# The mask term of 32 attention sets, added by two engines in place of one

## The chip, the cores and the metric

The kernel runs on one core of one Trainium2 chip. A core has five instruction queues that matter here: TensorE (PE, its weight loads are shown as PEld), VectorE (DVE), ScalarE (ACT), GpSimd (POOL) and SyncE (SP), which issues the DMAs. Each engine works through its queue in order; semaphores hold an instruction until what it needs is there. The metric is the device time of one execution in microseconds (us), as the median of several runs.

## The reference

Four cross-attention blocks follow each other on an array of 32 sequences, 64 rows each, 256 features. Blocks 0 to 2 are an 8-head attention without a mask, a 16-head attention with a boolean mask, and a latent attention with an integer mask and an MLP (those two masks come in through PE). Block 3 is a decoder layer: masked self-attention, masked cross-attention, and an MLP, all with 16 heads of 16 features. Only its two attentions use the mask in this form:

```python
def attention(q, k, v, mask):
    scores = jnp.einsum('bhqd,bhkd->bhqk', q, k) / jnp.sqrt(jnp.float32(HD))
    scores = scores * mask - 10000.0 * (1.0 - mask)
    probs = jax.nn.softmax(scores, axis=-1)
    return jnp.einsum('bhqk,bhkd->bhqd', probs, v)
```

The self-attention takes one mask of 64 x 64 for all sequences, the cross-attention one mask of 64 x 64 for each sequence. Everything is float32.

## The kernel before

Block 0 is written out by hand and runs until about 458 us. The three attentions after it and block 3's second one are cut into 80 *sets*: a set is two sequences (128 rows, on the partitions) with all 16 heads, or half the heads where the keys are twice as many. Sets 0 to 47 are of kind `k`, sets 48 to 63 of kind `s` (block 3's self-attention) and sets 64 to 79 of kind `x` (its cross-attention). Sets `s` and `x` are the masked ones, 32 in all.

`attend(n)` (line 1388) emits the work of set n. For a masked set this is: PE computes the scores into four PSUM banks (`a_scores`, tile `s`, of which there is one); DVE multiplies them by the mask on the way to SBUF (tile `E`, 128 x 1024, three of them), and POOL adds the second term, (mask - 1) x 10000, in place (`a_mask`, line 1026); DVE takes the largest of each row and head (`a_max`, tile `mx`); it is subtracted by DVE or POOL in turn (`a_sub`); ACT takes the exponential; DVE sums and inverts (`a_sum`, tile `sm`); PE turns the result, multiplies it with the values, and DVE scales the product (`a_fin`, tile `rb`), with ACT and POOL splitting it into a high and a low part (`xTho`, `xTlo`). The mask and its term are 64 columns wide and are read again for each of the 16 heads: `m3` and `c3` (tiles `m`, `c`) for kind `s`, computed once; `mk` and `ck` for kind `x`, loaded and computed for each set.

Between the sets, steps with due times prepare the keys, values and queries of later sets, the norms, the output projections, the MLP, and the weights (`norm_steps`, `mlp_steps`, `load_unit`). Some of them use DVE and POOL as well: `x<-pj,x` (adding a projection to the rows), `x<-x,row` (adding a bias row, POOL), `xTl`, `xTla`, `xTlh`, `xTln` (the low parts of transposed rows; DVE or POOL), `rstd` and `nmr` (norms, POOL), `w` and `wraw` (weights).

From set 0 on, the order of all instructions is computed when the kernel is built. Class `Plan` collects every operation, joins PE's neighbouring ones on one bank to *atoms*, and makes one atom of each operation of the other engines (`link`, line 254). `order` (line 289) then places the atoms one by one on the engine that can start first; where several could start, the smallest `urgent` goes first: the due time of the atom, plus a random number up to 0.5, less 3 for a DVE or ACT atom that reads PSUM. The random numbers are drawn one for each atom in the order of emission, from a fixed seed. The costs come from `cost` (line 194); of two lines that matter here the first is DVE's with both inputs in SBUF and the second is POOL's (w is the width in columns):

```python
return 0.3 + w * (1.05e-3 if o.method in ("tensor_copy", "tensor_scalar") else 1.3e-3), 0.05, None
...
return 0.1 + w * (2.45e-3 if three and not self.repeats(ins[1]) else 1.95e-3), 0.05, None
```

The operations are issued from one place (`write`, line 123), so in the profile almost all of them have line L125; L156 is the same for block 0. They are told apart by their tiles, written out<-in,in.

Of the kernel before, what the change touches and what calls it, by code (L numbers as in the profile page):

```python
# [15 lines left out]
ALU = mybir.AluOpType  # L16
# [3 lines left out]
P = 128  # L20
# [388 lines left out]
def mk_kernel(ctx: ExitStack, tc: tile.TileContext, a: dict, out: bass.AP):  # L409
    nc = tc.nc  # L410
    plan = Plan(dict(V=nc.vector, A=nc.scalar, G=nc.gpsimd, T=nc.tensor, S=nc.sync))
    V, A, G, T, SY = [plan.engine(k) for k in "VAGTS"]
# [613 lines left out]
    def a_mask(u):  # L1026
        if u["kind"] == "x":
            G.tensor_scalar(u["ck"], u["mk"], -1.0, 10000.0, ALU.add, ALU.mult)
        else:
            u["mk"], u["ck"] = m3, c3  # L1030
        spread = lambda t: t.unsqueeze(1).unsqueeze(1).broadcast_to([P, 4, 4, 64])
        V.tensor_tensor(u["ev"], u["src"], spread(u["mk"]), ALU.mult)
        G.tensor_tensor(u["ev"], u["ev"], spread(u["ck"]), ALU.add)
        u["src"] = u["ev"]

    def a_max(u):
# [351 lines left out]
    def attend(n):  # L1388

        for x in steps:  # L1390
            if x["due"] <= n:
                run(x)
        plan.due = n + 0.5
        for gen in loads.get(n, ()):
            next(gen)
        u = sets[n]
        for nme in (f"q{u['l']}{u['g']}", f"v{u['l']}{u['g']}" + ("1" if u["two"] else "")):
            run(by_name[nme])
        plan.due = n
        a_mask_load(u)  # L1400
        a_scores(u)
        if u["kind"] != "k":
            a_mask(u)
        a_max(u)
        a_sub(u)
        a_exp(u)
        a_sum(u)
        a_scale(u)
        a_rows(u)
        a_turn(u, 0)  # L1410
        a_turn(u, 1)
        a_values(u)
        a_fin(u)
# [261 lines left out]
```

## Time and profile before

| | |
|---|---|
| median of three runs | 1131.25 us (1130.16 to 1131.29) |
| the profiled execution | 1132.07 us |
| its span, first to last instruction | 1130.3 us |
| mean granted TensorE clock | 0.987 |
| busy: PE / PEld | 1067.8 (94%) / 872.2 us (77%) |
| busy: DVE / ACT / POOL | 894.9 (79%) / 906.3 (80%) / 761.8 us (67%) |
| POOL `E<-E,c` and `E<-E,ck`, 128 x 1024 | 16 and 16, median 2.38 and 2.39 us |
| DVE `E<-s,m` and `E<-s,mk`, 128 x 1024 | 16 and 16, median 1.22 and 1.21 us |

Busy time is the time in which an engine executes; it says nothing of the order. A group of the profile is all instructions with the same engine, operation, tiles and shape. "Idle before" is the time in which the engine stood still just before an instruction, with the engine that ended the wait. The chain of waits starts at the last instruction and goes back, at each step to what released it, so that it tells which engine set the time in each part of the span.

### The profile page before, as it was taken

Reading aid. Unit: us, or ns where it says so; the run is one execution under the profiler, and the core shown is the slowest. Engines: PE = TensorE matmul, PEld = TensorE weight load, DVE = VectorE, ACT = ScalarE, POOL = GpSimd, SP = SyncE. Lnnn points to the kernel's source line nnn. Section 1 sums busy time; section 2 is a strip of 40 time slices with the busy share of each in tenths; the row PEclk is TensorE's granted clock in tenths of the full one; section 3 lists DMA queues with packets and bytes.
Section 4 is the critical chain, followed back from the end, with each engine's and each line's share of the span. In section 5 each row is a group of like instructions: output and inputs, shape, how many; then the busy total and the mean of one; then the engine's idle time right before and its main releaser. Section 6 shows DMA issues by size and latency. Waiting matters only on the chain.

```text
span 1130.3 us, 35569 instructions
## 1 busy us (share of the span) xinstructions
PE 1067.8 (94%) x14396; PEld 872.2 (77%) x14396; DVE 894.9 (79%) x1575; ACT 906.3 (80%) x2326; POOL 761.8 (67%) x829
## 2 busy tenths in 40 slices
PE   6999999999999999899999999999999988889998
PEld 4666666666666666788898989998988877779998
DVE  4889989897888777688888878777878878777842
ACT  2888888887888789577778889889898777888974
POOL 3788888886778667635546634477866989996520
PEclk9999999999999999899999999999999989989999
DMA  3001211111110100311211100000000111110000
GB/s 96 21 25 36 61 35 49 35 34 44 34 34 25 34 16 2 93 37 58 68 47 47 34 26 26 21 29 22 21 20 21 49 51 51 43 34 21 11 20 29
DMA packets 41300, 41.21 MB, mean 36 GB/s; under 512 B 7059, under 2 KB 37796, under 8 KB 41136
## 3 DMA queue, kind: packets, MB, share of 16 engines
q1 hardware_dynamic: 40816, 38.54, 10.9%
q8 instruction: 114, 1.87, 0.7%
q10 hardware_dynamic: 320, 0.40, 0.1%
q14 instruction: 50, 0.41, 0.1%
HBM read 26.30 MB, written 2.10 MB: 25 GB/s over the span
## 4 chain that ended last, share of the span: by engine, by line
PE 59%; DVE 15%; ACT 10%; POOL 10%; issue 4%; DMA 0%; SPq 0%; DVEq 0%; POOLq 0%; ACTq 0%
PE pj L125 39%; PE pt L156 6%; ACT E L156 5%; PE av L156 5%; PE sc L156 4%; PE s L125 4%; DVE mx L156 3%; POOL E L125 3%; DVE E L125 2%; DVE PT L156 2%; ACT PT L156 2%; DVE sB L156 2%; POOL E L156 2%; DVE mx L125 2%; PE pt L125 1%
## 5 line engine op out<-in xcount | busy, mean ns | idle before, releaser
L156 POOL TENSOR_TENSOR E<-E,rs 128x512 f32<-128x512 f32 x256 | 263.5, 1040 | 84.0 <-DVE rs L156 64.5
L156 ACT ACTIVATE E<-sc,mx 128x256 f32<-128x256 f32 x512 | 238.4, 481 | 23.2 <-DVE rs L156 21.9
L156 DVE TENSOR_REDUCE mx<-sc 128x4 f32<-128x1024 f32 x128 | 155.8, 1217 | 2.8 <-PE sc L156 1.4
L156 PE MATMUL sc<-cd,T 64*128 64x256 f32 x1024 | 144.0, 400 | 10.5 <-ACT E L156 10.0
L125 POOL TENSOR_TENSOR E<-E,sm 128x512 f32<-128x512 f32 x96 | 101.1, 1078 | 68.9 <-DVE sm L125 56.1
L156 PE MATMUL av<-PT,us 128*64 128x256 f32 x1024 | 125.0, 385 | 0.0
L156 PEld LDWEIGHTS pt<-ident,E 64*128 64x128 f32 x2048 | 83.6, 139 | 43.6 <-POOL E L156 15.8
L156 PEld LDWEIGHTS av<-PT,us 128*64 128x64 f32 x1024 | 68.3, 136 | 54.7 <-issue 20.4
L156 PEld LDWEIGHTS sc<-cd,T 64*128 64x128 f32 x1024 | 89.6, 189 | 25.8 <-ACT E L156 17.8
L125 DVE TENSOR_REDUCE sm<-E 128x16 f32<-128x1024 f32 (+1 forms) x80 | 96.0, 1200 | 15.3 <-ACT E L125 15.3
L156 ACT ACTIVATION_READ_ACCUMULATOR E<-sc,mx 128x1 f32 x512 | 108.0, 211 | 0.0
L156 PE MATMUL pt<-ident,E 64*128 64x64 f32 x2048 | 98.2, 228 | 6.1 <-ACT PT L156 2.2
L125 ACT COPY PTe<-pj 128x512 f32<-128x512 f32 x160 | 88.0, 590 | 19.2 <-PE pj L125 17.1
L125 PE MATMUL pj<-ident,E 128*128 128x128 f32 x640 | 90.8, 281 | 8.0 <-DVE rb L125 2.5
L156 ACT COPY PT<-pt 128x512 f32<-128x512 f32 x128 | 75.6, 591 | 24.3 <-PE pt L156 22.8
L125 PE MATMUL pj<-w,xThh 128*128 128x256 f32 x512 | 93.4, 287 | 0.1
L125 PE MATMUL pj<-xThn,w 128*128 128x256 f32 x512 | 92.2, 285 | 0.7 <-DVE rb L125 0.4
L156 DVE COPY PT<-pt 128x512 f32<-128x512 f32 x128 | 86.0, 672 | 5.2 <-PE pt L156 5.1
L125 ACT ACTIVATE E<-E 128x1024 f32<-128x1024 f32 x80 | 84.9, 1062 | 5.8 <-DVE E L125 4.6
L125 PEld LDWEIGHTS pj<-ident,E 128*128 128x128 f32 x640 | 71.6, 143 | 16.7 <-issue 3.6
L125 DVE TENSOR_TENSOR xTlh<-u,xThh 128x512 fp32r<-128x512 f32 x64 | 54.8, 861 | 29.9 <-ACT xThh L125 29.5
L156 DVE RECIPROCAL rs<-sm 128x2 f32<-128x2 f32 x256 | 40.1, 156 | 46.5 <-ACT E L156 43.7
(223 smaller groups left out, 2798.3 us busy)
## 6 DMA issues: line engine op xcount, KB each, us to landing
kb<-kfm SPq DMA_DIRECT2D x44, 128.0 KB
xd<-in_x SPq DMA_DIRECT2D x32, 128.0 KB
cd<-in_ctx SPq DMA_DIRECT2D x32, 128.0 KB
boot<-in_ctxT SPq DMA_DIRECT2D x16, 256.0 KB
kb<-kfm SPq DMA_DIRECT2D x64, 64.0 KB
xt<-in_x SPq DMA_DIRECT2D x16, 128.0 KB
boot<-in_ctx SPq DMA_DIRECT2D x8, 256.0 KB
out<-x SPq DMA_DIRECT2D x8, 256.0 KB
```

The lines of the kernel that those rows point to most:

```text
L125: getattr(self.engines[o.key], o.method)(*[real(x) for x in o.p], **{k: real(x) for k, x in o.k.items()})
L156: return f(*p, **k)
```

## The change

The second term of the mask is added in two instructions in place of one. The tile `E` is seen as 4 groups x 4 heads x 64 keys, so its 1024 columns are divided by the first of these: the first three quarters, 768 columns, are added by POOL (`G`), and the last quarter, 256 columns, by DVE (`V`). DVE's instruction is emitted first. The multiplication before it and all else stay; the operation count grows by one DVE operation for each of the 32 masked sets.

```diff
-        spread = lambda t: t.unsqueeze(1).unsqueeze(1).broadcast_to([P, 4, 4, 64])
+        spread = lambda t, n=4: t.unsqueeze(1).unsqueeze(1).broadcast_to([P, n, 4, 64])
         V.tensor_tensor(u["ev"], u["src"], spread(u["mk"]), ALU.mult)
-        G.tensor_tensor(u["ev"], u["ev"], spread(u["ck"]), ALU.add)
+        V.tensor_tensor(u["ev"][:, 3:4], u["ev"][:, 3:4], spread(u["ck"], 1), ALU.add)
+        G.tensor_tensor(u["ev"][:, 0:3], u["ev"][:, 0:3], spread(u["ck"], 3), ALU.add)
         u["src"] = u["ev"]
```

## The prediction

> **What bounds the kernel now.** I read four views in this order: the page's busy shares, the busy times by stretch, the chain of work that ended last, and the groups and the timeline of the instructions that the change touches.
>
> The masked sets are the last 32 of the 80 sets that the planner orders, and their multiplications (DVE, `E<-s,m` and `E<-s,mk`) start between 785 and 1056 us. So I cut the end of the span into stretches, with one stretch of layer 0 to compare with. The columns are the stretch, its length, and busy us of PE, PEld, DVE, ACT and POOL.
>
> ```profile
> 60.00:250.00 190.00, 182.87 (x2003) 122.16 (x2003) 171.75 (x367) 160.85 (x558) 160.87 (x185) 1.00 0.14 41
> ...
> 785.00:880.00 95.00, 91.44 (x1387) 83.99 (x1370) 77.35 (x102) 84.16 (x169) 69.08 (x62) 1.00 0.05 19
> 880.00:990.00 110.00, 96.42 (x1376) 85.03 (x1374) 87.80 (x148) 86.68 (x185) 104.30 (x103) 0.93 0.16 50
> 990.00:1062.00 72.00, 68.42 (x915) 63.44 (x916) 58.19 (x72) 61.19 (x113) 54.70 (x49) 0.96 0.07 22
> ```
>
> The reader is to see three different limits. I call the last three rows A, B and C. In A, PE is busy 96% and is the limit; DVE is at 81%, POOL at 73%. In B, PE falls to 88% (13.6 us idle) and POOL is at 95%: B is bound by POOL. In C, PE is back at 95%. PE's idle time is 3.6 + 13.6 + 3.6 = 20.8 us: that is all that the change could ever win, since it takes nothing from PE. After 1062 us no masked set is left, and PE runs almost alone to the end.
>
> The chain of waits says the same of B. It runs mostly over POOL from 878.78 to 933.75 (with two turns over DVE and PE) and from 948.12 to 990.77 us; this is a piece of it (start, us, what):
>
> ```profile
> 961.50 2.40 POOL E L125
> 963.90 1.67 POOL xTlo L125
> 965.96 0.71 POOL rstdm L125
> 966.95 0.71 POOL rstda L125
> 967.74 0.50 POOL nmrm L125 x2
> 968.25 1.86 POOL E L125
> 970.20 0.25 POOL ck L125
> 970.52 2.38 POOL E L125
> 972.90 1.24 POOL x L125
> ```
>
> The 2.40 and the 2.38 are the additions that the change divides. Nine such additions of about 2.3 to 2.4 us, and one with 0.8 us of it, lie on these two runs of the chain.
>
> **The change part by part.** It edits one line, so every masked set (16 `s`, 16 `x`) is touched once: one POOL instruction becomes shorter, one DVE instruction is new, and the reduction `mx<-E` waits for both. No DMA, no tile and no PE work changes.
>
> *POOL, shorter.* Three rows of two-input POOL operations have three widths: `xTlo<-rb,xTho` 256 columns, median 0.74 us; `x<-x,row` 512 columns, 1.29 us; the addition itself, 1024 columns, 2.38 us (`c`) and 2.39 us (`ck`). They lie on a line of 2.15 ns a column, so 768 columns take 1.84 us. **Saved: 0.55 us a set**, 17.6 us for 32.
>
> *DVE, new.* The trace has no addition of 256 columns with both inputs in SBUF. `rb<-pj,rb` has this width with one input in PSUM: 0.41 us. DVE's two-SBUF-input `E<-E,mx` of 1024 columns takes 1.16 us when nothing is in its way, `xTlh` of 512 takes 0.68; that line also goes through 0.41. So 0.41 us undisturbed. But the same rows show that it will seldom be undisturbed:
>
> ```profile
> L125 DVE TENSOR_TENSOR E<-E,mx 128x1024 f32<-128x1024 f32 x16 | 30.2, 1890 | 0.3
> ```
>
> That is the group (16 instructions, 30.2 us busy, mean 1890 ns); and from the timeline (start, us, engine, operation):
>
> ```profile
> 808.48 3.45 DVE L125 TENSOR_TENSOR E<-E,mx 128x1024 f32<-128x1024 f32 x1
> ...
> 808.43 2.41 POOL L125 TENSOR_TENSOR E<-E,c 128x1024 f32<-128x1024 f32 x1
> ...
> 863.15 2.08 DVE L125 TENSOR_TENSOR E<-E,mx 128x1024 f32<-128x1024 f32 x1
> ...
> 864.11 1.73 POOL L125 TENSOR_TENSOR xTlo<-rb,xTho 128x256 fp32r<-128x256 f32 x1
> ```
>
> At 808.48 DVE starts a subtraction just after POOL's addition, and takes 3.45 us: the 2.36 us that POOL still ran, and then 1.09, its own undisturbed time. At 863.15 it waits 1.0 us for a POOL addition to end, runs 1.08, and now POOL's next instruction, started at 864.11, takes 1.73 in place of 0.74: it waited in turn. So where these two engines meet, a DVE operation with two SBUF inputs and a POOL operation run one after the other, and the later one stands at the head of its queue. The 16 `E<-E,mx` have a mean of 1.89 us, 0.73 us above the undisturbed one. That mean wait depends on POOL's instruction and not on DVE's width, so I give it to the new addition too: 0.41 + 0.73 = **1.14 us of DVE a set**. Ends: 0.41 when it runs first (it follows the multiplication on the same engine, while POOL's addition began 0.08 us after the multiplication's end in the sets where POOL was free); 0.41 + 1.84 = 2.25 when it always stands behind its own set's POOL addition. 1.14 is nearest to a measured row of the same operation kind.
>
> *POOL, waiting in return.* Each DVE addition holds POOL up to 0.41 us if POOL has something to run. In B it nearly always has (95%): 0.55 - 0.41 leaves 0.14 us a set. In A and C POOL has slack, and neither the gain nor the wait reaches the end.
>
> *A rule.* The Trainium skill, "GPSIMD Engine Reference", section Engine selection, puts elementwise work on VectorE because GpSimd is about twice as slow with two inputs; by that alone the sum would be the relief of the first rival below. The same page, section Key points, says that the two share SBUF interfaces and contend when a VectorE instruction has two SBUF inputs; it gives no price, this trace does (3.45 us against 1.16).
>
> *The new wait.* `mx<-E` now waits for two engines. Behind it in DVE's queue stand drains of PSUM (`rb`, `x<-pj,x`, `xTla`) for which ACT and then PE wait. In A and C the multiplication is followed on DVE by 3 to 12 other instructions before `mx<-E`, so DVE, not the addition's end, sets the time of most reductions there. A shorter addition wins nothing there.
>
> *The order.* The instruction order is computed: `cost` would now charge POOL 1.98 in place of 2.61 us and DVE 0.63 us more for the set (its formula gives 0.63 where I expect 1.14), and `order` draws one random tie-breaker for each atom, so every atom emitted after the first new one draws another number. Before 785 us the order stays almost as it is. The 346 us after it are re-dealt; I can't price that from the trace except by PE's idle time there, and I use it as width, some 3 us either way.
>
> *Sum by stretch.* A, 11 sets: DVE goes from 77.35 to 77.35 + 12.5 = 89.9 of 95 us, 95%. Two bounds: layer 0's stretch above has DVE at 90% beside PE at 96%, so nothing lost; B has an engine at 95% beside 12.3% of PE idle against A's 3.7%, so 8.2 us lost. I take a quarter of it, **+2.0**, because only 5 points of DVE separate A from the stretch that loses nothing. C, 7 sets: DVE 58.19 + 8.0 = 66.2 of 72, 92%; bounds 0 and (12.3 - 5.0)% of 72 = 5.3 us; a quarter, **+1.3**. B, 14 sets: POOL 14 x 0.14 = **-2.0** (ends: -7.7 without any wait, 0 with it and nothing saved on the chain). DVE gains 16.0 and stands at 103.8 of 110, 94%, as full as POOL is now. In its middle it is worse:
>
> ```profile
> 920.00:960.00 40.00, 33.82 (x562) 29.51 (x546) 33.97 (x55) 32.37 (x70) 38.96 (x36) 0.96 0.16 51
> ```
>
> Five multiplications start in these 40 us: DVE's 33.97 becomes 39.7 of 40. DVE has 6.0 us idle there, much of it waiting for others, and it works in order; I take 2.5 us of that as kept, **+2.5** (ends 0 and 6.0). Sum: 2.0 + 1.3 - 2.0 + 2.5 = **+3.8 us**. The profiled execution took 1132.07 (span 1130.3 and 1.77 around it), so 1135.9; it lay 0.8 above the median of the runs, 1131.25, so the forecast is **1135** for the median. About 0.2%, 2.3 us, is what a measurement of this kernel can tell from no change.
>
> **The rivals.**
> *POOL's relief decides.* For it: B's chain is POOL, and the additions on it are its longest pieces; if the DVE additions run first, in gaps, the chain loses 10 x 0.55 = 5.5 us (7.7 if all 14 count), and PE has 13.6 us idle there to give back. Against it: DVE meets POOL at work in B. 1131.25 - 5.5 = **1126**, 1122 to 1129. Chance 0.32.
> *No change.* PE in A and C hides everything, B's relief and DVE's load cancel: **1131**, 1129 to 1133.5. Chance 0.16.
> *DVE is stopped by its own set's addition.* Both halves become ready at the same moment. If POOL mostly starts first, a DVE addition takes 2.25 us, 72 us for 32, where DVE has 277 - 223.3 = 53.7 us idle from 785 to 1062. From about 1.7 us each (54 / 32) DVE alone is the bound of all three stretches: at 2.25 it is 18 us over, at 2.0 some 10. **1141** to 1149. Chance 0.12.
> *It doesn't do what it says.* POOL's time might not fall with the width; the three widths on one line speak against it. It is inside "no change".
>
> **How the numbers follow.** Forecast (slower, DVE's waits): 0.40, its own range 1133.5 to 1140. Faster is the first rival, 0.32. Within 0.2%: 0.16. Slower: 0.40 + 0.12 = 0.52. The range goes from 1123 (the first rival with most of its relief) to 1143 (the stopped DVE at its lower end), which leaves out about 0.15.
>
> **What would show it.** POOL's `E<-E,c` and `E<-E,ck` of 768 columns: 1.84 us when undisturbed, up to 2.25 behind DVE. The new DVE addition: a mean near 1.14, a smallest near 0.41. DVE in A near 90 us, POOL in B near 101. In the chain from 880 to 990, DVE where POOL stood. I am wrong if the new addition's mean is near 0.5 (then the first rival) or near 2 (then the last), or if PE's idle time in A and C doesn't grow although DVE does.

## The result and the profile after

The changed kernel takes 1138.78 us in the median of six runs (1136.13 to 1139.57), the kernel before 1131.51 in six runs beside them: a ratio of 1.0062, 95% interval 1.0051 to 1.0073. It is 7 us slower; the forecast was 4 us slower. The profiled execution took 1138.98 us with a span of 1137.3.

The stretches of the prediction, for the changed kernel (length, then busy us of PE, PEld, DVE, ACT, POOL, then the granted clock):

```profile
785.00:880.00 95.00, 89.64 (x1323) 81.32 (x1324) 85.20 (x117) 82.36 (x165) 64.25 (x65) 1.00 0.05 19
880.00:990.00 110.00, 97.16 (x1474) 85.38 (x1472) 99.34 (x147) 86.74 (x184) 101.74 (x100) 0.95 0.17 52
990.00:1062.00 72.00, 67.26 (x920) 60.98 (x912) 60.23 (x87) 59.65 (x116) 47.47 (x51) 1.00 0.06 18
1062.00:1138.00 76.00, 68.53 (x632) 66.74 (x620) 31.06 (x52) 45.18 (x88) 13.69 (x20) 0.94 0.06 22
```

DVE has 7.9, 11.5 and 2.0 us more than before in A, B and C, and POOL 4.8, 2.6 and 7.2 us less. PE idles 5.4, 12.8 and 4.7 us where it idled 3.6, 13.6 and 3.6. The stretches have fixed times and not the same work: what is not done in one comes in the next. In the last row, after the masked sets, PE is busy for 68.5 us and idle for 6.8 of the 75.3 us to the end of the span; before, it was busy for 64.5 and idle for 3.9 of 68.3:

```profile
1062.00:1131.00 69.00, 64.45 (x625) 63.31 (x623) 28.91 (x50) 42.39 (x87) 13.43 (x20) 0.98 0.07 24
```

The halves of the addition (smallest, median and largest time in ns of 16 each):

```profile
L125 POOL TENSOR_TENSOR E<-E,c x16: 1815/1853/2104, 787.7 to 917.7; 128x768 f32<-128x768 f32 x16
L125 DVE TENSOR_TENSOR E<-E,c x16: 384/443/1515, 788.4 to 907.1; 128x256 f32<-128x256 f32 x16
...
L125 DVE TENSOR_TENSOR E<-E,ck x16: 361/417/1873, 924.0 to 1065.7; 128x256 f32<-128x256 f32 x16
L125 POOL TENSOR_TENSOR E<-E,ck x16: 1810/1834/2206, 928.3 to 1059.1; 128x768 f32<-128x768 f32 x16
```

POOL's part takes the 1.84 us that were reckoned. DVE's part takes 0.42 to 0.44 in the median and up to 1.87; the two groups have means of 0.72 and 0.76 us. The page's sums agree: DVE 894.9 to 918.6 us (+23.7), POOL 761.8 to 746.9 (-14.9).

In B the chain still runs mostly over POOL (over DVE from 943.83 to 954.71). A piece of it (start, us, what):

```profile
928.39 1.77 POOL E L125
930.15 0.41 POOL nmra L125
930.57 0.69 POOL xTlo L125
931.26 1.23 POOL xTl L125
932.49 1.79 POOL E L125
934.28 1.68 POOL xTlo L125
935.96 3.67 POOL E L125 x2
```

The additions are shorter, and the 1.68 us of `xTlo` (0.74 alone) are a POOL instruction that stood behind a DVE subtraction (`E<-E,mx`, 1.72 us from 933.64 on).

### The profile page after: what moved, and what is told of

The parts are those of the page before. It is cut to its first block, busy times and chain, and to the rows that moved or that the text cites. A ratio compares the mean times of both kernels' runs of the same rounds, so it can differ in the third digit from the quotient of the medians.

```text
span 1137.3 us, 35626 instructions
## 1 busy us (share of the span) xinstructions
PE 1068.8 (94%) x14396; PEld 870.1 (77%) x14396; DVE 918.6 (81%) x1607; ACT 905.7 (80%) x2324; POOL 746.9 (66%) x829
## 3 DMA queue, kind: packets, MB, share of 16 engines
q8 instruction: 114, 1.87, 0.7%
## 4 chain that ended last, share of the span: by engine, by line
PE 52%; DVE 18%; ACT 13%; POOL 11%; issue 5%; DMA 0%; SPq 0%; DVEq 0%; POOLq 0%; ACTq 0%
PE pj L125 33%; PE pt L156 7%; ACT E L156 5%; PE av L156 5%; PE sc L156 4%; POOL E L125 3%; PE s L125 3%; DVE E L125 3%; DVE mx L156 3%; DVE PT L156 2%; ACT PT L156 2%; DVE sB L156 2%; POOL E L156 2%; DVE sm L125 1%; DVE mx L125 1%
## 5 line engine op out<-in xcount | busy, mean ns | idle before, releaser
L125 POOL TENSOR_TENSOR E<-E,sm 128x512 f32<-128x512 f32 x96 | 101.1, 1076 | 69.0 <-DVE sm L125 56.2
L156 PEld LDWEIGHTS av<-PT,us 128*64 128x64 f32 x1024 | 68.3, 136 | 54.8 <-issue 20.4
L125 DVE TENSOR_REDUCE sm<-E 128x16 f32<-128x1024 f32 (+1 forms) x80 | 95.9, 1199 | 15.1 <-ACT E L125 15.1
L125 PE MATMUL pj<-ident,E 128*128 128x128 f32 x640 | 93.0, 282 | 8.7 <-ACT PTe L125 4.6
L125 ACT COPY PTe<-pj 128x512 f32<-128x512 f32 x160 | 88.7, 590 | 14.6 <-PE pj L125 12.5
L156 ACT COPY PT<-pt 128x512 f32<-128x512 f32 x128 | 75.6, 591 | 25.3 <-PE pt L156 23.7
L125 PE MATMUL pj<-w,xThh 128*128 128x256 f32 x512 | 93.0, 287 | 1.7 <-ACT xThh L125 0.9
L125 ACT ACTIVATE E<-E 128x1024 f32<-128x1024 f32 x80 | 84.4, 1061 | 11.2 <-DVE E L125 7.1
L125 PE MATMUL pj<-xThn,w 128*128 128x256 f32 x512 | 90.8, 284 | 1.5 <-ACT PTe L125 0.7
L125 PEld LDWEIGHTS pj<-ident,E 128*128 128x128 f32 x640 | 71.4, 143 | 19.2 <-ACT PTe L125 5.9
L125 DVE TENSOR_TENSOR xTlh<-u,xThh 128x512 fp32r<-128x512 f32 x64 | 57.3, 899 | 30.2 <-ACT xThh L125 30.0
```

The lines of the kernel that those rows point to most:

```text
L125: getattr(self.engines[o.key], o.method)(*[real(x) for x in o.p], **{k: real(x) for k, x in o.k.items()})
L156: return f(*p, **k)
```

## The experiments

Theory W: the added DVE work costs more than POOL's relief brings, wherever the instructions stand. Theory O: the work is neutral or a gain, and the instruction order that the planner deals anew costs the time. To hold these apart, the first runs keep one of the two orders exactly: the planner sees the operations of one kernel, and only when an operation is written out is it exchanged, shortened, or left out. PE and ACT then have the same instructions in the same order as the kernel whose order is kept. (Helper lines shift in these kernels: L126 to L130 stand where L125 stood.)

**New order, old work.**

```diff
 V.tensor_tensor(u["ev"][:, 3:4], ...)
+plan.ops[-1].skip = True
 G.tensor_tensor(u["ev"][:, 0:3], ...)
+plan.ops[-1].full = (u["ev"], u["ev"], spread(u["ck"]), ALU.add)
```

> The instruction order that the change leads to, with the work of the kernel before: POOL adds all 1024 columns, and the 32 new DVE additions are left out when the order is written down; nothing else differs from the changed kernel on any engine. Theory W (the work costs: DVE's additions and their waits, as the prediction had it): without them the loss goes, 1130 to 1133 us. Theory O (the re-dealt order costs, the work itself is covered): it stays slow, 1137 to 1141 us, and POOL's longer additions may add to it. If both count, about 1135.

Measured: 1145.21 us, 1.0115 (1.0100 to 1.0130). Slower still than the changed kernel, at the old work: W by itself is refuted, since taking DVE's additions away and giving POOL its quarter back loses 6 us more (1.0115 against 1.0062). The new order is bad for the old work, by 13 us.

**Old order, new work, the quarter early.** The DVE addition is written when both the product and the term are.

```diff
-getattr(self.engines[o.key], o.method)(*[real(x) for x in o.p], ...)
+getattr(self.engines[o.key], o.method)(*[real(x) for x in getattr(o, "short", o.p)], ...)
+if getattr(o, "left", None):
+    o.left.remove(o)
+    if not o.left:
+        self.engines["V"].tensor_tensor(*[real(x) for x in o.quarter])
```

> The instruction order of the kernel before on every engine, with the work of the change: POOL adds 768 columns where it added 1024, and the DVE addition of 256 columns is put into DVE's queue as soon as the product and the term are both written (directly behind the multiplication in most sets). Theory W: it is slow like the changed kernel, 1135 to 1139 us. Theory O: the relief of POOL shows, with DVE's additions in the way of little: 1125 to 1131 us.

Measured: 1137.97 us, 1.0052 (1.0036 to 1.0068). As slow as the changed kernel without any new order, so O by itself is refuted as well. How a DVE addition costs PE's time is seen here; the lines are DVE's, then POOL's, ACT's and PE's own, of one moment (start, us, engine; in brackets the idle time before, and what ended it):

```profile
911.07 1.20 DVE L125 TENSOR_TENSOR E<-s,m 128x1024 f32<-128x1024 f32 x1
912.30 2.03 DVE L129 TENSOR_TENSOR E<-E,c 128x256 f32<-128x256 f32 x1
914.26 0.15 DVE L125 TENSOR_TENSOR b<-pj,vecs 128x1 f32<-128x1 f32 x1
...
912.25 1.80 POOL L125 TENSOR_TENSOR E<-E,c 128x768 f32<-128x768 f32 x1
...
915.68 0.58 ACT L125 CAST xTha<-pj 128x512 fp32r<-128x512 f32 x1 [2.18 <-PE pj L125]
...
914.55 1.09 PE L125 MATMUL pj<-ident,boot 128*128 128x128 f32 x4 [2.03 <-DVE b L125]
```

POOL had begun an addition of another set 0.05 us earlier. DVE's 256 columns stand behind it and take 2.03 us. Behind them in DVE's queue waits `b<-pj`, one column, that drains a PSUM bank; PE waits for the bank, 2.03 us, and ACT for PE. The DVE work that PE waits for is a trifle; its place in the queue is not.

**Old order, the quarter late.** As before, but the addition is written just ahead of the reduction that reads it.

```diff
 V.tensor_reduce(heads(u["mx"]), u["src"], AX.X, ALU.max, negate=True)
+plan.ops[-1].quarter = u["quarter"]
...
+if hasattr(o, "quarter"):
+    self.engines["V"].tensor_tensor(*[real(x) for x in o.quarter])
```

> As the run before, but the DVE addition stands directly ahead of the reduction that needs it, so that it often meets POOL's next instruction. Both theories: DVE's addition takes longer, 0.8 to 1.2 us in the mean, against 0.4 to 0.6 in the run before. Theory W: slower than that run by the 32 waits' share on the path, 2 to 8 us. Theory O: within 2 us of it.

Measured: 1132.79 us, 1.0006 (0.9991 to 1.0021): the change as a whole, with the quarter late, makes no loss that can be told from nothing. The early run's 32 additions took 0.82 us in the mean, these 0.78, so the theory that the waits' length decides was wrong (both theories had expected the late ones to be clearly longer). The same load, in the same order of all else, costs 5 us more in the early place than in the late one. PE's waits show a difference that fits (what PE waited for from 785 us on, then us in total, times, longest; the early run's lines are those with L125, the late run's those with L127):

```profile
PE pj L125 <- DVE b L125: 4.0, 2, 2.0
PE pj L125 <- DVE rb L125: 3.5, 4, 2.1
...
PE pj L125 <- DVE xTla L125: 2.5, 2, 1.7
...
PE pj L127 <- DVE rb L127: 3.6, 4, 1.4
...
PE pj L127 <- DVE xTla L127: 0.7, 1, 0.7
```

Altogether, waits for DVE to drain a PSUM bank hold PE for 13.1 us in the early run (11 waits), 6.8 in the late one (7) and 3.6 in the kernel before (4). One more thing differs: POOL's own additions have a median of 2.01 us in the early run, where DVE's often start first, and 1.83 to 1.84 in the late one. What that costs by itself was not tested.

**Old work, new draws.**

```diff
 at.urgent = at.due + ties.uniform(0, self.TIE) - ...
+if hasattr(at.ops[0], "burn"):
+    ties.uniform(0, self.TIE)
```

> The work of the kernel before, planned with the costs of before; only the random tie-breakers are drawn as in the changed kernel (one more draw behind each masked multiplication). Theory O in the form that the draws alone do it: 1136 to 1140 us. Theory O in the form that the planner's new costs do it, and theory W: 1130 to 1133 us. Any other time, say 1126 or 1134, tells how wide such re-dealing spreads by itself.

Measured: 1132.45 us, 1.0008 (0.9996 to 1.0019). These other tie-breakers alone change nothing that can be told from the noise.

**POOL's relief alone, old order.** Only `short`, with no DVE addition.

```diff
 G.tensor_tensor(u["ev"], u["ev"], spread(u["ck"]), ALU.add)
+plan.ops[-1].short = (u["ev"][:, 0:3], u["ev"][:, 0:3], spread(u["ck"], 3), ALU.add)
```

> The order of the kernel before on every engine; POOL adds 768 columns and nobody adds the last 256, so that quarter of the heads goes on without the mask's second term: the relief of POOL by itself, with no DVE addition. If POOL's shorter additions are worth what the prediction's first rival said, 1123 to 1127 us (the chain's ten additions at 0.55). If the chain over POOL is replaced at once by another limit, 1128 to 1131 us.

Measured: 1121.63 us, 0.9914 (0.9900 to 0.9929): 9.7 us faster. So POOL's relief is worth more than the first rival gave it. Its stretches:

```profile
785.00:880.00 95.00, 91.70 (x1370) 84.64 (x1368) 75.24 (x104) 84.31 (x170) 63.56 (x63) 1.00 0.05 19
880.00:990.00 110.00, 99.71 (x1413) 89.15 (x1412) 91.05 (x152) 90.68 (x191) 103.65 (x111) 0.94 0.17 55
990.00:1062.00 72.00, 69.80 (x975) 64.81 (x975) 55.83 (x75) 64.75 (x124) 50.20 (x48) 1.00 0.06 18
```

PE is busy 99.7 us in B (96.4 before) and 69.8 in C (68.4). Of the 9.6 us between the two profiled spans, 4.9 are PE's idle time from 785 us on and 4.7 its busy time, at a granted clock of 0.98 against 0.97; why the clock was higher is not shown.

This run is the measure for the two before it with DVE's additions in the same order: against it the additions cost 15.6 us early (0.9914 to 1.0052) and 10.4 us late (0.9914 to 1.0006). The late place is the cheaper one, not a free one: it uses up what POOL's relief brings.

**DVE's addition alone, old order and old work.** It reads the term twice and writes a dead tile.

```diff
 V.tensor_tensor(u["ev"], u["src"], spread(u["mk"]), ALU.mult)
+side = c3.unsqueeze(1).broadcast_to([P, 4, 64])
+plan.ops[-1].side = (spare.rearrange("p (h k) -> p h k", k=64), side, side, ALU.add)
```

> The order and all the work of the kernel before, and directly behind each of the 32 masked multiplications a DVE addition of 256 columns with both inputs in SBUF, which reads the mask's term and writes a tile that nobody reads: DVE's load, and its meeting with POOL, by themselves, with no new wait for anybody's result. Theory W (DVE's load and waits cost): 1135 to 1139 us, some 4 to 7 above before. Theory P (the place and the waits for the term cost, not the load): 1131 to 1133 us.

Measured: 1143.35 us, 1.0106 (1.0091 to 1.0122): 12 us slower, with no new wait for anybody's result. Theory W had 4 to 7. Of the 10.9 us between the profiled spans, 8.5 are idle time of PE. The difference is not that of the clock: executions of the kernel before with a mean granted clock of 0.984 to 0.986, beside this run, took 1131.1 to 1133.7 us, and those of this run with 0.985 took 1142.9. PE is busy less in all three stretches:

```profile
785.00:880.00 95.00, 89.29 (x1347) 81.97 (x1345) 80.63 (x111) 82.67 (x165) 68.42 (x60) 1.00 0.05 19
880.00:990.00 110.00, 94.08 (x1347) 83.27 (x1346) 99.54 (x153) 79.42 (x169) 100.42 (x93) 0.91 0.15 47
990.00:1062.00 72.00, 65.63 (x825) 59.96 (x824) 61.14 (x73) 60.03 (x115) 57.64 (x59) 0.95 0.08 26
```

**New work, old draws.**

```diff
-at.urgent = at.due + ties.uniform(0, self.TIE) - ...
+at.urgent = at.due + (self.TIE / 2 if hasattr(at.ops[0], "new") else ties.uniform(0, self.TIE)) - ...
```

> The changed kernel, planned with its own costs, but each old atom keeps the tie-breaker that it had before, and the new atoms get a fixed one in the middle. If the re-dealt draws make the loss, 1130 to 1133 us; if the planner's new costs and the new atoms' place make it, 1136 to 1140 us. The run of the old work with the new draws (1.0008 of before) speaks for the second.

Measured: 1137.70 us, 1.0047 (1.0030 to 1.0064); two of the nine executions, at a mean granted clock of 0.992, took 1132.3 and 1132.7 us, the others, at 0.986 to 0.989, 1137.2 to 1139.1. The draws are not the cause here either.

**New order, relief alone.** The `skip` of the first run without its `full`.

> The order of the changed kernel on every engine, POOL with 768 columns, and the DVE additions left out, so that the last quarter of the heads goes without the mask's second term. Against the changed kernel (1.0062 of before) it prices DVE's additions within the new order. Theory W: 1129 to 1133 us, so the additions cost 6 to 9 us. Theory O (the order costs): 1135 to 1138 us, so the additions cost 1 to 3.

Measured: 1133.16 us, 1.0016 (1.0007 to 1.0026). By the ratios, DVE's additions cost 5 us in the new order (1.0016 to 1.0062), and POOL's relief is worth 11 (1.0115 to 1.0016). The order alone, at this work, costs 11.5 us (0.9914 to 1.0016).

**Old prices.** The planner charges POOL's part 2.61 us and DVE's nothing.

```diff
 t, late, form = self.cost(o)
+t = getattr(o, "price", t)
```

> The changed kernel, planned with other prices: POOL's addition of 768 columns is charged what the 1024 were (2.61 us) and DVE's addition nothing, and each old atom keeps its old tie-breaker. PE, ACT and POOL then have the order of the kernel before, and the planner puts the DVE addition where it likes. If the new prices make the order slow (as the draws do not), 1132 to 1135 us, like the late quarter; if the DVE addition at the planner's place is what costs, 1136 to 1139 us.

Measured: 1135.96 us, 1.0047 (1.0032 to 1.0062), between the two expectations in time and not to be told from the new prices' 1.0047. The order of PE, ACT and POOL is that of before, and the DVE addition stands where the planner likes it, mean 0.97 us. So most of the loss needs no new order.

**Early quarter without the wait for the term.**

```diff
-o.left, o.quarter = left, (..., spread(u["ck"], 1), ALU.add)
+o.left, o.quarter = left, (..., spread(c3, 1), ALU.add)
```

> The run with the old order and the quarter directly behind the multiplication, but in the 16 cross-attention sets the quarter takes the self-attention's term, which is there from the start, so that DVE waits for no POOL result (the mask's term of that quarter is that of the wrong mask). If DVE's wait behind POOL's backlog for the term is what sets the early quarter (1.0052) apart from the late one (1.0006), 1132 to 1135 us; if it is the early place itself (both halves start together, and POOL's addition starts later), 1136 to 1139 us.

Measured: 1139.76 us, 1.0083 (1.0068 to 1.0098). My idea that DVE waited for POOL's late terms fell: without that wait it is no faster, if anything slower. So it is the early place itself; DVE's PSUM drains hold PE for 11.9 us here, as in the early run.

**No addition: the product computed with a shift, old order, and the same planned anew.**

```diff
-V.tensor_tensor(u["ev"], u["src"], spread(u["mk"]), ALU.mult)
-G.tensor_tensor(u["ev"], u["ev"], spread(u["ck"]), ALU.add)
+for r in range(4):
+    V.scalar_tensor_tensor(u["ev"][:, r], u["src"][:, r], 128.0, u["mk"].unsqueeze(1).broadcast_to([P, 4, 64]), ALU.add, ALU.mult)
```

> No addition at all, old order: DVE computes (score + 128) x mask in four instructions of 256 columns out of PSUM in place of the one multiplication, and POOL's addition and its term's computation are left out. For a mask of zeros and ones the softmax is the same, since a constant in all scores cancels and a masked score stands at least 128 below the others' shift; for other masks it would differ. POOL loses 2.4 us a set and DVE gains some 0.2 (4 x 0.33 against 1.22). The run with POOL's relief alone gained 9.7 us for 0.55 us a set and left 15.8 us of PE idle time after 785 us: 1113 to 1121 us. If DVE's extra 0.2 us count as its additions did, 1119 to 1124.

> The same computation, planned anew with its own prices. The change's own re-planned order cost 12 to 14 us against the old one at equal work without DVE's additions, so this may lie anywhere from 1112 to 1130 us; below the old order's time if the planner uses POOL's free time well.

Measured: 1123.21 us, 0.9940 (0.9923 to 0.9956) in the old order, and 1139.63 us, 1.0079 (1.0060 to 1.0098) planned anew. The first beats both kernels, by 0.6% and, by the two ratios, 1.2%. It takes all 2.4 us of each addition from POOL and is no faster than the relief of 0.55 (1121.6), so another limit follows soon. The second has the same operations in another order and lies outside what I had expected (1112 to 1130), 16 us above the first. The first kernel's DVE groups (count, then busy us and mean ns), and its rows for A and B:

```profile
L126 DVE SCALAR_TENSOR_TENSOR E<-s,m 128x256 f32<-128x256 f32 x64 | 22.6, 415 | 5.6 <-PE s L130 5.5
L126 DVE SCALAR_TENSOR_TENSOR E<-s,mk 128x256 f32<-128x256 f32 x64 | 22.5, 413 | 4.8 <-PE s L130 4.6
```

```profile
785.00:880.00 95.00, 91.80 (x1386) 84.61 (x1368) 74.01 (x140) 84.10 (x170) 42.82 (x52) 1.00 0.05 19
880.00:990.00 110.00, 100.64 (x1482) 89.00 (x1487) 95.90 (x191) 92.51 (x196) 81.50 (x93) 0.97 0.18 55
```

In B, POOL is busy 81.5 us of 110 in place of 104.3, and PE 100.6, hardly more than with the relief alone (99.7): POOL is the limit no longer. With 256 columns, one input in PSUM and one in SBUF, DVE needs 0.41 us in the mean; the change's additions, of the same width with both inputs in SBUF, needed 0.72 and 0.76. In the kernel that was planned anew one wait of PE stands out (start, us, PE's operation, and the idle time before it):

```profile
996.44 0.90 PE L125 MATMUL pj<-ident,boot 128*128 128x128 f32 x3 [5.21 <-ACT boot L125]
```

The chain leads back to the norm's small POOL instructions (`rstdm`, `nmrm`, `nmra`), which that order had put too late. Its granted clock is lower as well (0.979 over the span against 0.992). Of the 20.7 us between the two profiled spans, 8.5 are idle time of PE from 785 us on and 12.2 its busy time, at a clock of 0.95 against 0.99. That the order lowers the clock is not shown, but the medians of four executions each lie 16 us apart, and none of the second kernel's had a mean clock above 0.984, none of the first's one below 0.989.

## Why the prediction was right, and where it was not

The direction holds, and the time lies inside the range: +3.8 us were forecast, +7.3 measured, about twice as much. The terms hold less well than the sum, and that the sum came out this near is in good part luck.

**POOL's part**, 1.84 us: measured 1.85 and 1.83. Right.

**DVE's part**, 0.41 undisturbed and 1.14 in the mean: 0.42 to 0.44 in the median and 0.74 in the mean of all 32. That DVE's addition waits for POOL is right, the mean too high by half; DVE in A came to 85.2 us, where near 90 was forecast. I gave the new addition the mean wait of `E<-E,mx`, but the planner puts it at other moments: 18 of the 32 took less than 0.45 us, so nothing held them. With the right number the sum would have been smaller, and the prediction worse; the next point says why.

**The price of DVE's time.** I summed +2.0 (A), +1.3 (C) and +2.5 (B), 5.8 us for 36.5 us of DVE. DVE's addition alone costs 12.0 us for some 26 us of it (32 instructions, mean 0.81). The step that failed is "a quarter of it", the place between the two bounds: I asked how full DVE becomes. The runs show that with nearly the same load the additions cost 10.4 us (late quarter) or 15.6 (early) against the relief alone, so the change as a whole costs 0.7 us or 5.9 in the old order, by what stands behind the waiting instruction. One moment is shown above: a PSUM drain, for which PE waits. The sums of PE's waits for such drains, 13.1 us early, 6.8 late and 2.6 with the relief alone, agree with it; that each of the 32 additions works in this way was not shown. (Between 920 and 960 us six multiplications start, not five; the addition of the sixth, from 959.44, comes later, so the term is as it was.)

**POOL's relief**, -2.0: it alone brings -9.7. Mis-sized by a factor of five, and my upper end for it, 7.7, was too small also. I had set it to nothing in A and C, because PE is 95 to 96% busy there, and had let DVE's holding of POOL eat three quarters of it in B. Measured, PE gains in A (91.4 to 91.7), in B (96.4 to 99.7) and in C (68.4 to 69.8). The bound of 20.8 us, PE's idle time, was not a bound either: half of the relief's gain in the profiled execution was PE's busy time. Both wrong terms have opposite signs, and a good part of the error cancelled: in the old order relief and early addition by themselves make -9.7 + 12.0 = +2.3, and together +5.9 to +9.4. So the two don't simply add.

**By stretch**: PE's idle time grew by 1.8 us in A (+2.0 forecast) and 1.2 in C (+1.3), and fell by 0.7 in B (+0.5). That A and C agree is luck: the terms behind them are off by the factors above, and a stretch doesn't hold the same work in both kernels. The tail after 1062 us, to which I gave nothing, has the most: PE's idle time grew by 2.9 us there and its busy time by 4.1. That is not work left over, for after its last scores PE has 689 instructions in both kernels. In the changed kernel's profiled execution they meet a stretch of 6.8 us, from 1071.2 on, at a granted clock of 0.50. From 785 us to the end the clock is 0.97 in both; PE's idle time makes 5.1 of the 7.0 us between the two spans there, and its busy time 1.9. Where the clock falls may differ between executions, and only one of each kernel has a profile, so how much of the busy time belongs to the change stays open.

**The order**, "some 3 us either way": failed as a size. The draws alone give 1 us; but the whole new order, at equal work, costs 11.5 to 13 us, and the shifted product differs by 16 between two orders. In the change itself it shows little (1.0062 against 1.0047 with PE's, ACT's and POOL's old order, within the intervals), because DVE's additions cost 5 us in the new order and 15 in the old one at the planner's place (0.9914 to 1.0047). So it depends on what is changed first how the 7 us are divided: the new work in the old order costs 5.3 (old prices), and the new order then 1.7; the new order with the old work costs 13, and the new work then takes 6 off. Where the new order costs time is seen in PE's waits for `PTe`, which ACT copies out of PSUM (from 785 us on; the kernel before, the changed kernel, the new order with the relief alone, and with the old work):

```profile
PE pj L125 <- ACT PTe L125: 2.9, 5, 1.2
...
PE pj L125 <- ACT PTe L125: 8.1, 10, 1.9
...
PE pj L127 <- ACT PTe L127: 7.6, 10, 1.4
...
PE pj L127 <- ACT PTe L127: 8.6, 13, 1.9
```

These waits come with the order, with DVE's additions or without. Where the 5 us of the additions go in the changed kernel itself stays open: DVE's PSUM drains hold PE for only 2.1 us there.

**The chain** in B: I expected DVE where POOL stood. It is still mostly POOL, whose busy time in B, 101.7 us, is the 101 that was forecast. DVE's share shows as 11 us of the chain (943.83 to 954.71) and as POOL instructions that wait (the 1.68 us above).

**The rivals**: the relief is real, as the first rival said, and is paid away. The third, DVE always behind its own set's addition (2.25 us), didn't happen: the largest is 1.87.

## What to carry to other kernels

When work is moved from a full engine to a second one, price both sides by runs that do one side alone in the unchanged order, and then both together; a sum can be near while both terms are wrong. Ask not how full the second engine becomes but what stands behind the new instruction in its queue: ahead of the operation that needs it, it cost 10 us, as much as the relief brought, and right behind its input 16 to 19. Where a planner deals the order, keep the old order beside the new one: the same computation lay 16 us apart between two orders, part of it at a lower granted clock.

## What the runs showed of the hardware

A DVE operation with two SBUF inputs and a wide two-input POOL operation ran one after the other (2.03 us for 256 columns behind a POOL addition of 1.80), while the same width with one input in PSUM kept 0.41 us: 39 of the 128 shifted products began beside a wide two-input POOL operation, and none of these took more than 0.43. Not every POOL operation holds DVE: the prediction's "a POOL operation" was too wide. In the changed kernel's timeline two additions, 0.80 us together, ran beside a one-input POOL operation that had begun before them, and neither side was held (DVE's line and POOL's):

```profile
906.73 0.80 DVE L125 TENSOR_TENSOR E<-E,c 128x256 f32<-128x256 f32 x2
...
906.44 0.92 POOL L125 TENSOR_SCALAR boot<-boot,vecs 128x256 f32<-128x256 f32 x1
```

Nor did POOL's `rstda`, two inputs of two columns (0.71 us): in the late quarter's run, an addition that began at 971.23, 0.36 us after it, took 0.42. The other way round a one-input POOL operation did wait: in the changed kernel `wraw<-wraw,vecs`, 0.92 us alone, began at 895.04, just behind a DVE subtraction of two SBUF inputs (`E<-E,mx`, 894.97, 1.22 us), and took 1.94.

The Trainium skill, "GPSIMD Engine Reference", section Key points, names just the two-SBUF-input operations (and the two-port modes) as those that contend; the 128 shifted products, mean 0.41, against the 32 additions, mean 0.74, agree with it.

I had not expected how soon the relief of POOL ends: 0.55 us less for each set brought 9.7 us, all 2.4 us less, with some 0.2 us more on DVE, brought 7. What limits B after the first 0.55 us was not tested. In the relief's run POOL is still busy for 103.7 of the 110 us, but 42.5% of its chain from 880 to 990 us lie on PE's `pj`. The longest piece there that is not PE's (start, us, what) is a weight that arrives late:

```profile
917.74 4.52 DMA wraw<-in_L_w
...
922.29 0.62 ACT w L125
...
922.93 0.84 ACT qfm L125 x2
923.77 0.95 ACT E L125
...
924.77 1.83 PE pj L125 x8
```

ACT stands in order behind the weight's conversion, and with it an exponential for which PE idles 3.48 us. In the chain the DMA follows POOL's last reading of the raw tile (`w`, which ends at 917.71), so this looks like POOL's lateness still, handed on over a buffer.
